# Layer 1 self-attention: the fourth of a head's products with the values issued behind the next head's first scores

## The chip, the cores and the metric

The kernel runs on one core of a Trainium2 chip. The metric is the device time of one execution in microseconds (us). The core has five engines with an instruction queue each: TensorE for matmuls (PE in the profile, its weight loads PEld), VectorE (DVE), ScalarE (ACT), GpSimd (POOL) and SyncE (SP), which issues most of the transfers. The engines run side by side and wait for each other by semaphores.

## The reference, cut to what matters

The program is a two-layer decoder on 4 batches of 512 rows of 512 columns, in float32. Each layer has a self-attention, a cross-attention and a feed-forward part, and each part is added to the rows and followed by a normalisation of the row. The change is in the self-attention of layer 1, which has 16 query heads of 128 columns, four of which share one key and value head, a rotation of queries and keys by position, and a causal mask:

```python
    xqkv = x @ Wqkv
    xq, xk, xv = ...                 # 16 query heads, 4 key and 4 value heads of 128
    xq = apply_rotary_emb(xq)
    xk = apply_rotary_emb(xk)
    scores = jnp.einsum('bqhd,bkhd->bhqk', xq, xk) * scale
    scores = scores + causal_add[None, None]
    probs = jax.nn.softmax(scores, axis=-1)
    attn = jnp.einsum('bhqk,bkhd->bqhd', probs, xv).reshape(B, S, q_size)
    return attn @ Wo
...
    x = _layernorm(x + _L1_attn_ref(x, L1_attn_Wqkv, L1_attn_Wo), axis=-1)
```

## The kernel before, in words

`l1_attn` walks over 64 heads, numbered n = 0 to 63 (batch n // 16, head h = n % 16). Three heads are in work at a time. In the turn of head n the loop writes, for i = 0 to 3: the scores of one block of 128 query rows of head n + 1 (`scores`, L918 to L922: a matmul into `ps_s`, the mask and the row maximum on DVE, the exponential on ACT), one of four products that make the query of head n + 2 (`queries`, L905), the transposes of one block of 128 key columns of head n's probabilities (`turn`, L935, copied out of `ps_t` into `PT` by ACT at L940 for even blocks and by DVE at L938 for odd ones), and the division of head n + 1's finished rows by their sums (`normalise`, L928 and L929). Behind the last query product stands the rotation of that query (`rope`): three DVE instructions, L875 to L877, and one on POOL, L878, which writes `q`.

Then comes `values(n, pts)`: four products of the transposed probabilities with the values, accumulated in one `ps_m` buffer (L950). Causality makes them 512, 384, 256 and 128 columns wide. The fourth, of 128 columns, reads the `PT` block that DVE copies last. ACT copies the sum into the tile `attnT` (L952). When h % 4 is 3, the four heads in `attnT` are multiplied by their part of `Wo` and added to the rows: 16 matmuls of 512 columns, at L160 in the helper `mm`, and four additions at L292. At the start of the turn of head n the loop writes `keys(n + 2)`, which does four matmuls (also at L160) and a rotation if n + 2 is the first of a group of four, and nothing otherwise. So between the turns of head n and n + 1 there stands, besides `values`: nothing more when n % 4 is 0 or 2, the keys of head n + 3 when it is 1, and the projection when it is 3. I call these plain heads, key heads and projection heads. After the last head of a batch come `layernorm(b)` and the values of the next batch (`prep_values`, 16 matmuls at L160, copies at L890).

A float32 matmul of 512 columns shows as two MATMUL records of about 0.43 us each in sequence, and one of 128 columns as two of about 0.11 us.

What sets the order on the engines: from the end of the layer 0 feed-forward until the call of `finish(3)` after head 2, the order on PE, DVE and ACT is the written one (`in_order`, L834). From there to the end of `l1_attn` a planner orders each engine's instructions when the program is built: on each engine it takes, of those that by its own estimate of durations are ready, the one that is written first. The engines then execute that order strictly; the chip does not choose again. The buffers concerned: `ps_m` 3, `ps_s` 3, `ps_t` 2, `PT` 6, `P` 8, `attnT` 1, `tmp` 4.

`at_start` runs `finish(1)` to `finish(3)` after heads 0 to 2 (the ends of the layer 0 feed-forward: scaling on ACT at L841 and on DVE at L842, transposes at L846, a projection, a `layernorm`), and `at_end` runs `begin(0)` to `begin(4)` after heads 59 to 63, which loads and prepares the cross-attention.

Of the kernel before, what the change touches and what calls it, by code (L numbers as in the profile page):

```python
# [17 lines left out]
P = 128  # L18
B, S, F = 4, 512, 512
# [67 lines left out]
def decoder_kernel(ctx: ExitStack, tc: tile.TileContext, a: dict, out: bass.AP):  # L87
# [21 lines left out]
    V, A, G, PE = nc.vector, nc.scalar, nc.gpsimd, nc.tensor  # L109


    def act(tag, free, bufs=1, dtype=F32):
        return ap.tile([P, *free], dtype, tag=tag, name=tag, bufs=bufs)

    def tmp(dtype=F32):
        return tp.tile([P, 512], dtype, tag="tmp", name="tmp")

    def small(n, tag, bufs=2):
        return sp.tile([P, n], F32, tag=tag, name=tag, bufs=bufs)

    def prob(tag, free, bufs, dtype=F32):
        return pools["pp"].tile([P, *free], dtype, tag=tag, name=tag, bufs=bufs)

    def pss():
        return pools["ps_s"].tile([P, 512], F32, tag="s", name="ps_s")
# [6 lines left out]
    def psm(dtype=F32):  # L132
        return pools["ps_m"].tile([P, 512], dtype, tag="m", name="ps_m")
# [7 lines left out]
    def load(src, free):  # L141

        w = weight(free)
        nc.sync.dma_start(w, src)
        return w

    def rows(w):
        return w.rearrange("(k p) n -> p k n", p=P)

    def tk(t):  # L150
        return slice(t * P, (t + 1) * P)
# [4 lines left out]
    def mm(ps, lhs, rhs):  # L156

        n = len(lhs)
        for i, (x, y) in enumerate(zip(lhs, rhs)):
            PE.matmul(ps, lhsT=x, rhs=y, start=(i == 0), stop=(i == n - 1))  # L160
# [54 lines left out]
    def layernorm(b):  # L215
        mv = small(8, "mv")
        for i in range(4):
            st = sp.tile([P, 6], F32, tag="bn", name="bn")
            V.bn_stats(st, X[4 * b + i])  # L219
            V.bn_aggr(mv[:, 2 * i:2 * i + 2], st)  # L220
        rstd = small(4, "rstd")
        A.activation(rstd, mv.rearrange("p (t s) -> p t s", s=2)[:, :, 1], AF.Sqrt, bias=LN_EPS)  # L222
        V.reciprocal(rstd, rstd)
        for i in range(4):
            x = X[4 * b + i]
            V.tensor_scalar(x, x, mv[:, 2 * i:2 * i + 1], rstd[:, i:i + 1], ALU.subtract, ALU.mult)  # L226
# [60 lines left out]
    def add_projection(b, lhs, rhs):  # L287

        for t in range(4):
            ps = psm()  # L290
            mm(ps, [x[:, tk(t)] for x in lhs], rhs)
            V.tensor_tensor(X[4 * b + t], X[4 * b + t], ps, ALU.add)  # L292

    def chunks(w):
        return [w[:, k, :] for k in range(w.shape[1])]
# [565 lines left out]
    def l1_attn(at_start, at_end):  # L861
        cos, sin = prob("cos", [S], 1), prob("sin", [S], 1)
        nc.sync.dma_start(cos, a["k_rope"][0])
        nc.sync.dma_start(sin, a["k_rope"][1])
        wqkv = rows(a["L1_attn_Wqkv"])
        wk = load(wqkv[:, :, 4 * F:5 * F], (4, F))
        wv = load(wqkv[:, :, 5 * F:6 * F], (4, F))
        wq, wo = [None] * 4, [None] * 4
        for of, g in ((wq, 0), (wq, 1), (wo, 0), (wq, 2), (wo, 1), (wq, 3), (wo, 2), (wo, 3)):
            src = wqkv[:, :, g * F:(g + 1) * F] if of is wq else rows(a["L1_attn_Wo"])[:, 4 * g:4 * g + 4, :]  # L870
            of[g] = load(src, (4, F))

        def rope(dst, ps, scale):
            x, y = tmp(), tmp()
            V.scalar_tensor_tensor(x, ps, scale, cos, ALU.mult, ALU.mult)  # L875
            V.scalar_tensor_tensor(y[0:64], ps[64:128], scale, sin[64:128], ALU.mult, ALU.mult)
            V.scalar_tensor_tensor(y[64:128], ps[0:64], scale, sin[0:64], ALU.mult, ALU.mult)  # L877
            G.tensor_tensor(dst, x, y, ALU.add)  # L878

        heads = [(b, h) for b in range(B) for h in range(H1)]
        st, qs, ks, ps_q, ps_sm = {}, {}, {}, {}, {}

        def prep_values(b):
            v = prob("v", [4, F], 1)
            for t in range(4):
                ps = psm()
                mm(ps, [st["xt"][:, k, tk(t)] for k in range(4)], chunks(wv))
                A.copy(v[:, t, :], ps)  # L890
            st["v"] = v

        def keys(n):
            b, h = heads[n]
            if h % 4 == 0:
                ps = psm()
                mm(ps, [wk[:, k, tk(h // 4)] for k in range(4)], chunks(st["xt"]))
                ks[b, h // 4] = prob("k", [S], 3)
                rope(ks[b, h // 4], ps, 1.0)

        def queries(n, i):
            b, h = heads[n]
            if i == 0:
                ps_q[n] = psm()
            PE.matmul(ps_q[n], lhsT=wq[h // 4][:, i, tk(h % 4)], rhs=st["xt"][:, i, :],  # L905
                      start=(i == 0), stop=(i == 3))
            if i == 3:
                qs[n] = prob("q", [S], 3)
                rope(qs[n], ps_q.pop(n), float(D1) ** -0.5)

        def scores(n, qi):
            b, h = heads[n]
            w, q, k = (qi + 1) * P, qs[n], ks[b, h // 4]
            if qi == 3:
                ps_sm[n] = [None] * 4, small(4, "sums", 3), small(4, "nmax", 3)
            probs, sums, nmax = ps_sm[n]
            s = pss()
            PE.matmul(s[:, :w], lhsT=q[:, tk(qi)], rhs=k[:, :w], start=True, stop=True)  # L918
            V.tensor_tensor(s[:, tk(qi)], s[:, tk(qi)], causal_mask, ALU.add)
            V.tensor_reduce(nmax[:, qi:qi + 1], s[:, :w], AX.X, ALU.max, negate=True)  # L920
            p = probs[qi] = prob("P", [S], 8)
            A.activation(p[:, :w], s[:, :w], AF.Exp, bias=nmax[:, qi:qi + 1],  # L922
                         accum_out=sums[:, qi:qi + 1])

        def normalise(n, qi):
            probs, sums, _ = ps_sm[n]
            p, w = probs[qi], (qi + 1) * P
            V.reciprocal(sums[:, qi:qi + 1], sums[:, qi:qi + 1])  # L928
            V.tensor_scalar(p[:, :w], p[:, :w], sums[:, qi:qi + 1], None, ALU.mult)  # L929

        def turn(n, c):
            probs = ps_sm[n][0]
            pt = pst()
            for qi in range(c, 4):
                PE.transpose(pt[:, tk(qi)], probs[qi][:, tk(c)], ident)  # L935
            sb = prob("PT", [S], 6)
            if c % 2:
                V.tensor_copy(sb[:, c * P:], pt[:, c * P:])  # L938
            else:
                A.copy(sb[:, c * P:], pt[:, c * P:])  # L940
            return sb

        def values(n, pts):
            b, h = heads[n]
            g = h // 4
            if h % 4 == 0:
                st["ft"] = act("attnT", [4, S])
            av = psm()
            for c in range(4):
                PE.matmul(av[:, c * P:], lhsT=st["v"][:, c, tk(g)], rhs=pts[c][:, c * P:],  # L950
                          start=(c == 0), stop=(c == 3))
            A.copy(st["ft"][:, h % 4, :], av)  # L952
            if h % 4 == 3:
                add_projection(b, chunks(st["ft"]), chunks(wo[g]))
            del ps_sm[n]

        N = len(heads)
        st["xt"] = transposed(0)
        for n in range(2):
            keys(n)  # L960
            for i in range(4):
                queries(n, i)
        for qi in (3, 2, 1, 0):
            scores(0, qi)
        prep_values(0)
        for qi in (3, 2, 1, 0):
            normalise(0, qi)
        for n, (b, h) in enumerate(heads):
            pts = []
            if n + 2 < N:  # L970
                keys(n + 2)
            for i in range(4):
                qi = 3 - i
                if n + 1 < N:
                    scores(n + 1, qi)
                if n + 2 < N:
                    queries(n + 2, i)
                pts.append(turn(n, i))
                if n + 1 < N and i:
                    normalise(n + 1, qi + 1)  # L980
            values(n, pts)
            if n + 1 < N:
                normalise(n + 1, 0)
            if h == 13 and b + 1 < B:
                st["xt"] = transposed(b + 1)
            if n < 3:
                at_start(n)
            if n >= N - 5:
                at_end(n - N + 5)
            if h == 15:  # L990
                layernorm(b)
                if b + 1 < B:
                    prep_values(b + 1)

# [438 lines left out]
```

## Time and profile before

| what | value |
|---|---|
| median of three runs | 2961.57 us (2957.27 to 2965.47) |
| the profiled execution | 2978.49 us, its span 2976.7 us |
| mean granted TensorE clock | 0.979 |
| PE busy | 2800.3 us, 94% of the span |
| DVE / ACT / POOL busy | 1770.5 / 1059.2 / 337.5 us |
| the stretch of `l1_attn` with the planner's order, 1110 to 1930 us | 820 us, PE busy 803.26, DVE 558.32, ACT 238.75, POOL 88.60 |

The span runs from the first to the last instruction; the profiled execution is 1.8 us longer than its span. Times in a timeline are us from the start of the span. In a row of the timeline there stand the start, the duration, the engine, the line of the code, the operation, what it writes and reads, the count of merged instructions and, in brackets, how long the engine was idle before it and what ended that. PE's matmul durations overlap, so a group's place in time says more than its length.

### The profile page before, as it was taken

Reading aid. Unit: us, or ns where it says so; the run is one execution under the profiler, and the core shown is the slowest. Engines: PE = TensorE matmul, PEld = TensorE weight load, DVE = VectorE, ACT = ScalarE, POOL = GpSimd, SP = SyncE. Lnnn points to the kernel's source line nnn. Section 1 sums busy time; section 2 is a strip of 40 time slices with the busy share of each in tenths; the row PEclk is TensorE's granted clock in tenths of the full one; section 3 lists DMA queues with packets and bytes.
Section 4 is the critical chain, followed back from the end, with each engine's and each line's share of the span. In section 5 each row is a group of like instructions: output and inputs, shape, how many; then the busy total and the mean of one; then the engine's idle time right before and its main releaser. Section 6 shows DMA issues by size and latency. Waiting matters only on the chain. (4 is left out here: it accounts for less than half of the span.)

```text
span 2976.7 us, 30405 instructions
## 1 busy us (share of the span) xinstructions
PE 2800.3 (94%) x11514; PEld 1353.3 (45%) x11514; DVE 1770.5 (59%) x3586; ACT 1059.2 (36%) x1945; POOL 337.5 (11%) x295
## 2 busy tenths in 40 slices
PE   8999999998997989999999999999998999998888
PEld 3444444564563445545555555543333343333443
DVE  4565455543111577766766767656666666564898
ACT  2343342333221222322332322234554544544444
POOL 3000000042004001101111111121211211100000
PEclk9999999999999999999999999999999999999999
DMA  9600000004303020000000000100111010010000
GB/s 383 272 15 0 18 11 14 22 32 143 132 33 114 29 71 1 1 1 1 1 1 0 1 29 22 57 22 29 43 36 43 29 42 23 1 43 1 15 15 29
DMA packets 56453, 131.85 MB, mean 44 GB/s; under 512 B 4809, under 2 KB 24026, under 8 KB 50146
## 3 DMA queue, kind: packets, MB, share of 16 engines
q1 hardware_dynamic: 53218, 121.31, 11.3%
q0 software_dynamic: 3072, 8.39, 0.8%
q8 instruction: 99, 1.62, 0.2%
q14 instruction: 64, 0.52, 0.1%
HBM read 82.76 MB, written 46.92 MB: 44 GB/s over the span
## 5 line engine op out<-in xcount | busy, mean ns | idle before, releaser
L160 PE MATMUL ps_m<-w,attnT 128*128 128x512 f32 (+2 forms) x1216 | 443.2, 515 | 11.8 <-DVE x L292 6.1
L1138 DVE TENSOR_REDUCE maxes<-ps_b 128x2 f32<-128x1024 f32 x256 | 312.0, 1223 | 237.6 <-PE ps_b L1150 212.1
L1154 ACT ACTIVATE PT<-ps_b 128x1024 f32<-128x1024 f32 x256 | 260.7, 1022 | 243.6 <-PE ps_b L1150 241.5
L1150 PE MATMUL ps_b<-q,k 32*128 32x512 f32 x1024 | 293.0, 650 | 16.6 <-DVE maxes L1138 8.5
L1134 PE MATMUL ps_b<-k,q 32*128 32x512 f32 x1024 | 286.4, 644 | 2.3 <-ACT PT L1154 1.8
L160 PEld LDWEIGHTS ps_m<-w,attnT 128*128 128x128 f32 x960 | 182.4, 193 | 189.7 <-issue 171.1
L905 PE MATMUL ps_m<-xT,w 128*128 128x512 f32 x512 | 261.4, 594 | 0.0
L292 DVE TENSOR_TENSOR x<-x,ps_m 128x512 f32<-128x512 f32 x128 | 87.7, 687 | 290.9 <-PE ps_m L160 263.1
L922 ACT ACTIVATE P<-ps_s,nmax 128x512 f32<-128x512 f32 (+3 forms) x256 | 135.2, 528 | 234.4 <-DVE nmax L920 233.4
L918 PE MATMUL ps_s<-k,q 128*128 128x512 f32 (+3 forms) x512 | 184.2, 443 | 18.7 <-POOL q L878 17.1
L878 POOL TENSOR_TENSOR q<-tmp 128x512 f32<-128x512 f32 x64 | 81.2, 1269 | 766.7 <-DVE tmp L877 732.1
L950 PE MATMUL ps_m<-PT,v 128*128 128x512 f32 (+3 forms) x512 | 162.8, 441 | 3.6 <-DVE PT L938 3.6
L349 ACT ACTIVATE P<-ps_s,nmax 128x512 f32<-128x512 f32 x128 | 88.4, 692 | 203.6 <-DVE nmax L347 203.6
L1134 PEld LDWEIGHTS ps_b<-k,q 32*128 32x128 f32 x1024 | 79.0, 185 | 164.4 <-issue 116.5
L929 DVE TENSOR_SCALAR P<-P,sums 128x512 f32<-128x512 f32 (+3 forms) x256 | 150.3, 587 | 5.3
L160 PE MATMUL ps_m<-w,xT 128*128 128x512 f32 (+1 forms) x384 | 143.6, 529 | 3.5 <-DVE v L317 3.5
L1161 PE MATMUL ps_m<-PT,vv 128*32 128x512 f32 x1024 | 139.9, 619 | 4.8 <-ACT PT L1154 4.8
L935 PEld LDWEIGHTS ps_t<-kc,P 128*128 128x128 f32 x640 | 83.9, 141 | 120.7 <-issue 81.7
L950 PEld LDWEIGHTS ps_m<-PT,v 128*128 128x128 f32 x512 | 89.3, 191 | 105.9 <-issue 49.4
L327 PE MATMUL ps_m<-xT,w 128*128 128x512 f32 x256 | 121.3, 600 | 10.9 <-DMA w<-in_L_attn_Wq 10.9
L920 DVE TENSOR_REDUCE nmax<-ps_s 128x1 f32<-128x512 f32 (+3 forms) x256 | 125.5, 490 | 5.6
L160 PE MATMUL ps_m<-xT,w 128*128 128x256 f32 (+1 forms) x384 | 126.6, 469 | 0.8 <-DVE x L292 0.8
(269 smaller groups left out, 4254.7 us busy)
## 6 DMA issues: line engine op xcount, KB each, us to landing
hidden<-w SPq DMA_DIRECT2D x16, 1024.0 KB, 16.9
result<-w SPq DMA_DIRECT2D x16, 1024.0 KB, 16.8
w<-in_L_ffn_gateT SPq DMA_DIRECT2D x8, 1024.0 KB, 4.7
w<-in_L_ffn_upT SPq DMA_DIRECT2D x8, 1024.0 KB, 4.8
w<-in_L_ffn_downT SPq DMA_DIRECT2D x8, 1024.0 KB, 5.0
w<-in_L_attn_Wqkv SPq DMA_DIRECT2D x6, 1024.0 KB, 5.2
w<-in_L_attn_Wo SPq DMA_DIRECT2D x5, 1024.0 KB
result<-P SPq DMA_DIRECT2D x18, 256.0 KB, 2.1
```

The source lines that it names most:

```text
L160: PE.matmul(ps, lhsT=x, rhs=y, start=(i == 0), stop=(i == n - 1))
L905: PE.matmul(ps_q[n], lhsT=wq[h // 4][:, i, tk(h % 4)], rhs=st["xt"][:, i, :], start=(i == 0), stop=(i == 3))
L918: PE.matmul(s[:, :w], lhsT=q[:, tk(qi)], rhs=k[:, :w], start=True, stop=True)
L920: V.tensor_reduce(nmax[:, qi:qi + 1], s[:, :w], AX.X, ALU.max, negate=True)
L922: A.activation(p[:, :w], s[:, :w], AF.Exp, bias=nmax[:, qi:qi + 1], accum_out=sums[:, qi:qi + 1])
L929: V.tensor_scalar(p[:, :w], p[:, :w], sums[:, qi:qi + 1], None, ALU.mult)
L950: PE.matmul(av[:, c * P:], lhsT=st["v"][:, c, tk(g)], rhs=pts[c][:, c * P:], start=(c == 0), stop=(c == 3))
L1134: PE.matmul(s[:, j, :], lhsT=q[strip(i), tk(qi)], rhs=k[strip(i), :], start=True, stop=True)
L1138: V.tensor_reduce(at[:, 2 * half:2 * half + 2, 16 * (1 - g % 2)], s, AX.X, ALU.max, negate=True)
L1150: PE.matmul(s[:, j, :], lhsT=k[strip(i), tk(c)], rhs=q[strip(i), :], start=True, stop=True)
L1154: A.activation(p, s, AF.Exp)
L1161: PE.matmul(avs[g][strip(i), :], lhsT=vv[c][:, 4 * m + i, 16 * par:16 * par + 32], rhs=pts[g, c, i // 2][:, i % 2, :], start=(c == 0), sto ...
```

## The change

`values` becomes a generator. Its first call does the products c = 0, 1 and 2 and stops. The rest (the fourth product, the copy into `attnT`, the projection where h % 4 is 3, and after the last head of a batch the `layernorm` and the values of the next batch) is written in the next head's turn, at i = 0, behind `keys` and the first `scores`, and ahead of the first query product. For head 63 it follows at once. The `attnT` tile is asked for behind the fourth product instead of ahead of the first. No instruction is added or removed.

```diff
         def values(n, pts):
             b, h = heads[n]
             g = h // 4
+            av = psm()
+            for c in range(4):
+                if c == 3:
+                    yield
+                PE.matmul(av[:, c * P:], lhsT=st["v"][:, c, tk(g)], rhs=pts[c][:, c * P:],
+                          start=(c == 0), stop=(c == 3))
             if h % 4 == 0:
                 st["ft"] = act("attnT", [4, S])
-            av = psm()
-            for c in range(4):
-                PE.matmul(av[:, c * P:], lhsT=st["v"][:, c, tk(g)], rhs=pts[c][:, c * P:],
-                          start=(c == 0), stop=(c == 3))
             A.copy(st["ft"][:, h % 4, :], av)
             if h % 4 == 3:
                 add_projection(b, chunks(st["ft"]), chunks(wo[g]))
+            if h == 15:
+                layernorm(b)
+                if b + 1 < B:
+                    prep_values(b + 1)
             del ps_sm[n]
...
+        rest = iter(())
         for n, (b, h) in enumerate(heads):
...
                 if n + 1 < N:
                     scores(n + 1, qi)
+                if i == 0:
+                    next(rest, None)
                 if n + 2 < N:
                     queries(n + 2, i)
...
-            values(n, pts)
+            rest = values(n, pts)
+            next(rest)
             if n + 1 < N:
                 normalise(n + 1, 0)
+            else:
+                next(rest, None)
...
-            if h == 15:
-                layernorm(b)
-                if b + 1 < B:
-                    prep_values(b + 1)
```

## The prediction, made before the change was run

> **What bounds the kernel now.** I read the page first, then the chain of waits of PE, then the timeline of one plain head, one projection head and two single places. From the page:
>
> ```profile
> PE 2800.3 (94%) x11514; PEld 1353.3 (45%) x11514; DVE 1770.5 (59%) x3586; ACT 1059.2 (36%) x1945; POOL 337.5 (11%) x295
> ...
> L918 PE MATMUL ps_s<-k,q 128*128 128x512 f32 (+3 forms) x512 | 184.2, 443 | 18.7 <-POOL q L878 17.1
> ...
> L950 PE MATMUL ps_m<-PT,v 128*128 128x512 f32 (+3 forms) x512 | 162.8, 441 | 3.6 <-DVE PT L938 3.6
> ```
>
> PE is the bound: whatever leaves PE idle or fills its holes moves the end. The wait that the change would cover, that of the fourth product for its `PT` block, is worth 3.6 us of idle PE in all; the scores' wait for the rotated query is worth 17.1. The waits from 990 to 1950 us (engine, line, what it waited for: us, times, longest) say the same in another way:
>
> ```profile
> PEld ps_m L950 <- DVE PT L938: 39.4, 62, 1.8
> ...
> PEld ps_s L918 <- POOL q L878: 23.7, 31, 1.0
> ...
> PE ps_s L918 <- POOL q L878: 17.1, 31, 0.6
> ...
> PE ps_m L950 <- DVE PT L938: 3.6, 6, 1.0
> ```
>
> The weight load waits 62 times for `PT`, but PE itself only 6 times. Why, a plain head (n = 32) shows:
>
> ```profile
> 1532.31 2.10 PE L950 MATMUL ps_m<-PT,v 128*128 128x512 f32 x6
> ...
> 1534.24 1.02 PE L905 MATMUL ps_m<-xT,w 128*128 128x512 f32 x2
> 1534.59 0.29 DVE L938 COPY PT<-ps_t 128x128 f32<-128x128 f32 x1
> 1534.73 1.26 POOL L878 TENSOR_TENSOR q<-tmp 128x512 f32<-128x512 f32 x1 [34.99 <-DVE tmp L877]
> ...
> 1535.10 0.38 PE L950 MATMUL ps_m<-PT,v 128*128 128x128 f32 x2
> ...
> 1536.05 1.12 PE L918 MATMUL ps_s<-k,q 128*128 128x512 f32 x2 [0.56 <-POOL q L878]
> ```
>
> Three products, then the next head's first query product (L905, written later, put ahead by the planner), then the fourth product, then the scores. Counted from the end of the third product (1534.24): `PT` is ready at 0.64, the query product ends at 0.86, so the fourth product starts at once and ends at 1.08. POOL ends at 1.75 and the scores start at 1.81. The hole is 1.81 - 1.08 = 0.73 us, and it belongs to `q`. The projection head n = 39 has no hole, since the projection covers `q` (ready at 1621.36 + 1.27 - 1620.64 = 1.99):
>
> ```profile
> 1620.64 1.02 PE L160 MATMUL ps_m<-w,attnT 128*128 128x512 f32 x2
> ...
> 1621.57 0.49 PE L950 MATMUL ps_m<-PT,v 128*128 128x128 f32 x2
> ...
> 1621.89 13.04 PE L160 MATMUL ps_m<-w,attnT 128*128 128x512 f32 x30
> ...
> 1634.77 1.02 PE L918 MATMUL ps_s<-k,q 128*128 128x512 f32 x2
> ```
>
> **What the Trainium skill says.** "TensorE: Matmul & The Clock Gate", Architectural detail: PE's queue can pull weight loads ahead of running matmuls, while ACT and DVE are strictly first in, first out. The trace agrees: the load of the fourth product waits 0.50 us for `PT` while PE works, and no matmul overtakes another. "GPSIMD Engine Reference", 3.1 Elementwise: a two-input add takes 4497 ns for 2048 elements; a quarter of that is 1.12 us as an estimate, the trace has 1.26 for 512, and that is used. The same page, 1 Specifications: POOL's SBUF interface is shared with VectorE; the division of 256 columns (L929) beside L878 takes 1.34 us against 0.35 elsewhere, yet L878 stays at 1.26, so `q` isn't made later by it.
>
> **The change, part by part.** No instruction is added or taken away, and none of the moved ones issues a DMA; SP's queue waits for nothing here that comes later. The question is only the new order on PE, and whether the planner holds the scores ready earlier than the chip does.
>
> It does. At head 2 DVE has the mask of the next scores ahead of the scaling L842:
>
> ```profile
> 1077.96 1.70 ACT L841 ACTIVATE w<-w,share 128x256 f32<-128x256 f32 x4
> ...
> 1079.23 0.30 DVE L919 TENSOR_TENSOR ps_s<-ps_s,kc 128x128 f32<-128x128 f32 x1 [0.67 <-PE ps_s L918]
> ...
> 1079.43 1.66 DVE L842 SCALAR_TENSOR_TENSOR w<-w,share 128x256 f32<-128x256 f32 x4
> ```
>
> L842 is written earlier, and on the chip its first input was ready at 1077.96 + 0.43 = 1078.39, 0.84 us before the mask could start. The planner put it second, so in its plan `q` comes at least some 0.8 us earlier against the chain `PT`, fourth product, L952, L841 than on the chip (1.11 after `PT`), so within some 0.3 to 0.4 of `PT`. That supposes that the scaled rows' gather is not late in the plan. And when is `PT` ready in the plan? At head 61 five transposes of 0.11 us, which are written later, stand ahead of the fourth product, so at about 0.44 to 0.55 behind the third (0.90 on the chip; key and projection heads run 0.23 later than plain ones). So planned `q` is at about 0.5 to 0.7 in a plain head and 0.6 to 0.95 in a projection head, as estimates. Behind the third product neither the scores nor the fourth product is planned ready, so the filler stays: the query product or the first projection matmul, to 0.86. Then the planner chooses, and now the scores are written first.
>
> - Plain heads from n = 4 to 60, 29 of them: query product, scores, fourth product. The scores can't start before 1.81 whatever stands ahead. The fourth product leaves the hole, where it cost nothing, and its 0.22 us goes behind the scores, ahead of the work that leads to the next query. 29 x 0.22 = +6.4 us.
> - Projection heads, n = 3 to 59, 15 of them: the scores move from behind the projection into it. From the end of the third product to that of the scores and all 16 projection matmuls PE has 16 x 0.86 + 0.22 + 0.86 = 14.84 us of work, and took 1634.77 + 0.86 - 1620.64 = 14.99. With the scores at 0.86 PE waits until 1.99 + 0.05 = 2.04, 1.18 us instead of 0.15: +1.03. With the fourth product first (it ends at 1.14) it waits 0.90 + 0.06: +0.81. I take 0.9: 15 x 0.9 = +13.5 us.
> - Key heads, n = 5 to 61, 15 of them: the four key matmuls (3.44 us) cover both `PT` and `q`. Before, the scores started 3.82 behind the third product, with 3.66 of work: 0.16 idle. That goes: -2.4 us.
> - Heads 0 and 1, in the written order: the fourth product waited while PE would be idle for L842 anyway (1.69 and 1.74 us), so leaving costs and gains nothing there. But the copy into `attnT` is now queued on ACT between the exponential of the first scores and the `PT` copy that PE awaits (1044.26 and 1071.71, PE idle 3.32 and 1.89 us): 0.48 us each, +1.0 us. Head 2's fourth product is free of the written order; nothing.
> - `layernorm` and `prep_values` inside the generator, three times: the same instructions behind one score block. The square root's table load and the one back (1.28 us each) are one pair as before and lie beside 13.8 us of PE work; without that cover 3 x 1.28.
> - Buffers: the sum in `ps_m` is held up to 2 us longer. The other two are the next query's sum and one that the rotation has left by then (L877 ends at 0.5 to 0.75), so nothing waits; if PE did wait for a slot it would be for the rest of L877, under 0.1 us a head, either way inside the range. `attnT` asked for later: nothing, since its readers ended a head earlier.
>
> Sum: 6.4 + 13.5 - 2.4 + 1.0 = +18.5 us. Against the profiled execution: 2978.49 + 18.5 = 2997.0. That execution stands 0.57% above the median of the runs; the addition is the same there, so I forecast 2961.57 + 18.5 = 2980 us.
>
> **The rivals.**
>
> 1. The planner's `q` is later than I infer, over 0.86 in plain and over 1.14 in projection heads. Then plain heads stay as they are, and in projection heads another projection matmul fills to 2.0, when `q` is there. Left: -2.4 + 1.0, that is 2960 us. For it: only the bound of 1.08 for plain heads is firm, since nothing was put between the fourth product and the scores. Against it: head 2. Here the change doesn't do what it says.
> 2. In between: `q` planned at 0.86 to 1.08, plain heads stay, projection heads put the scores behind the fourth product: 15 x 0.81 - 2.4 + 1.0 = +10.8, 2972 us.
> 3. Faster: with neither the scores nor the fourth product planned ready at 0.86, a second query product (0.86 us) goes into the plain heads' hole, which then is 1.81 - 0.86 = 0.95 wide. It would save 0.73 us in 29 heads, 21 us, 2940 us; it decides from 13 heads on (8.9 / 0.73). For it: the hole is there, and the product needs nothing but `xT` and weights. Against: before, the fourth product was always chosen at 0.86, so it was planned ready.
> 4. Slower still: DVE's load shifts and the planner puts the 256-column division ahead of the rotation in plain heads too, as it does in the others (0.23 us later): 29 x 0.23 = +6.7 on top, 2987 us.
>
> **How the numbers follow.** A measurement can tell about 0.3%, 8.9 us, from no change: 2952.7 to 2970.5. Forecast with either order in projection heads (2976 to 2983): 0.52. Rival 1: 0.21. Rival 2: 0.11, of which a fifth may fall within 0.3%. Rival 3: 0.11. Rival 4: 0.05. So slower 0.66, same 0.23, faster 0.11. The range takes the forecast and rivals 1, 2 and most of 4, with the run to run spread of 4 us: 2956 to 2988; the slower cases alone span 2968 to 2988.
>
> **What the profile after would show.** In plain heads L918 ahead of the 128-column L950, with an idle time of about 0.95 us before it, and that head longer by 0.22. In projection heads L918 behind one L160 matmul, idle for 0.9 to 1.2 us, and the sum of the waits of L918 for `q` up from 17 us to some 30 (its own part of the hole, without the weight load's). Key heads: L160 times 8 without the L950 between. The idle before L950 for `PT` at almost nothing. The prediction is wrong if in the projection heads L918 still comes late enough for `q`, or if a longer filler than one matmul stands ahead of it.

## The result and the profile after

The changed kernel is slower: 2989.0 us median against 2961.48 (a fourth run of the kernel before has joined the three of the table), a ratio of 1.0087 with a 95% interval of 1.0074 to 1.0100, so about 26 us, and 27.5 by the medians.

The two profiled executions differ by only 12.4 us (spans 2976.7 and 2989.1). The one of before took 21 us longer up to the first product of head 0 (1019.54 against 998.11 us), in work that the change doesn't touch; in the runs below this part takes 994 to 1019 us. From there to the first product of head 63 (1960.87 and 1966.86) the stretch went from 941.33 to 968.75 us: +27.4, which is what the medians show. What follows took 6.4 us longer after the change (1022.2 against 1015.8); it takes 1015 to 1026 us in the runs below, so that isn't told from noise. All comparisons of traces below are made inside this stretch.

Inside the stretch PE was busy 911.3 us before and 911.8 after, at a mean granted clock of 0.99 both times, so the loss is idle time of PE, and its waiting for `q` grew. The rows of the page after that answer to the three shown of before:

```profile
PE 2801.1 (94%) x11492; PEld 1356.9 (45%) x11514; DVE 1777.7 (59%) x3586; ACT 1054.6 (35%) x1945; POOL 338.4 (11%) x295
...
L918 PE MATMUL ps_s<-k,q 128*128 128x512 f32 (+3 forms) x512 | 185.4, 445 | 45.2 <-POOL q L878 43.6
...
L950 PE MATMUL ps_m<-PT,v 128*128 128x512 f32 (+3 forms) x512 | 159.8, 436 | 0.0
```

The fourth product's wait for `PT` went from 3.6 us to nothing; the scores' wait for `q` went from 17.1 to 43.6. The waits from 990 to 1985 us (engine, line, what it waited for: us, times, longest):

```profile
PEld ps_s L918 <- POOL q L878: 81.0, 49, 2.1
...
PE ps_s L918 <- POOL q L878: 43.4, 49, 1.3
```

They were 31 waits before (one of them ahead of head 0) and are 49 now: the 15 projection heads have joined, and with them the key heads n = 13, 29 and 45 and head 61. The plain head n = 32 and the projection head n = 39 in the timeline:

```profile
1525.66 2.10 PE L950 MATMUL ps_m<-PT,v 128*128 128x512 f32 x6
...
1527.59 1.02 PE L905 MATMUL ps_m<-xT,w 128*128 128x512 f32 x2
1527.94 0.29 DVE L938 COPY PT<-ps_t 128x128 f32<-128x128 f32 x1
1528.08 1.26 POOL L878 TENSOR_TENSOR q<-tmp 128x512 f32<-128x512 f32 x1 [36.11 <-DVE tmp L877]
...
1529.40 1.13 PE L918 MATMUL ps_s<-k,q 128*128 128x512 f32 x2 [0.78 <-POOL q L878]
...
1530.36 0.39 PE L950 MATMUL ps_m<-PT,v 128*128 128x128 f32 x2
```

```profile
1616.09 1.02 PE L160 MATMUL ps_m<-w,attnT 128*128 128x512 f32 x2
1616.67 0.29 DVE L938 COPY PT<-ps_t 128x128 f32<-128x128 f32 x1
1616.81 1.26 POOL L878 TENSOR_TENSOR q<-tmp 128x512 f32<-128x512 f32 x1 [8.87 <-DVE tmp L877]
...
1618.12 1.13 PE L918 MATMUL ps_s<-k,q 128*128 128x512 f32 x2 [1.01 <-POOL q L878]
1619.09 0.38 PE L950 MATMUL ps_m<-PT,v 128*128 128x128 f32 x2
```

In the plain head `PT` is ready 0.63 us behind the third product (1527.60) and PE is free at 0.86, but the scores are next in its queue, and it waits for `q` until 1.80 with the fourth product, which could run, standing behind them. In the projection head the same wait lasts from 1616.95 to 1618.12. The fourth product could have run in it (`PT` is there at 1616.96), and so could the next two projection matmuls of 0.86 us, which read earlier heads in `attnT`. Of all 16 only the four that multiply head 39 itself need the fourth product first.

Measured from the first product of one head to that of the next, the heads fall into a few groups, and within a group they agree to 0.02 us, head 42 aside (0.48):

| heads | scores start behind the third product, before and after | change per head | sum |
|---|---|---|---|
| plain, all others (18) | 1.80, 1.80 | +0.22 | +3.9 |
| plain, behind one of the 11 key heads below (11) | 1.80, 2.03 | +0.45 | +5.0 |
| projection, n = 7 to 59 (14), and n = 3 | 14.13 (27.86 at a batch's end), 2.03; at n = 3 15.27, 2.30 | +1.11, +0.32 | +15.8 |
| key (11) | 3.82, 3.43 | -0.17 | -1.9 |
| key at n = 13, 29, 45 (3) | 5.99, 2.04 | +0.68 | +2.0 |
| n = 61, and n = 0 to 2 | 4.62, 2.07 at n = 61 | | +0.6, +2.0 |

The sums make the 27.4 us. In the three key heads of the fifth row the scores now stand among transposes of the next batch's rows (L233), and wait; in head 13:

```profile
1225.53 1.13 PE L918 MATMUL ps_s<-k,q 128*128 128x512 f32 x2 [0.45 <-POOL q L878]
```

### The profile page after: what moved, and what is told of

It reads as the page before. It is cut to its first block, busy times and chain, and to the rows that moved or that the text cites. A ratio compares the mean times of both kernels' runs of the same rounds, so it can differ in the third digit from the quotient of the medians.

```text
span 2989.1 us, 30383 instructions
## 1 busy us (share of the span) xinstructions
PE 2801.1 (94%) x11492; PEld 1356.9 (45%) x11514; DVE 1777.7 (59%) x3586; ACT 1054.6 (35%) x1945; POOL 338.4 (11%) x295
## 5 line engine op out<-in xcount | busy, mean ns | idle before, releaser
L918 PE MATMUL ps_s<-k,q 128*128 128x512 f32 (+3 forms) x512 | 185.4, 445 | 45.2 <-POOL q L878 43.6
L919 DVE TENSOR_TENSOR ps_s<-ps_s,kc 128x128 f32<-128x128 f32 x256 | 75.3, 295 | 127.1 <-PE ps_s L918 127.1
L954 ACT COPY attnT<-ps_m 128x512 f32<-128x512 f32 x64 | 37.4, 585 | 296.3 <-PE ps_m L950 296.3
L940 ACT COPY PT<-ps_t 128x512 f32<-128x512 f32 (+1 forms) x128 | 61.2, 478 | 218.7 <-PE ps_t L935 218.7
```

## The experiments

Two theories. The order theory: only the place on PE matters; the scores, which stand in PE's order earlier than the chip has `q`, are now ahead of work that could fill the wait. The holding theory: the sum in `ps_m` is held longer and the copy into `attnT` and all behind it come later, and each postponed head pays for that alike, 27.5 / 63 = 0.44 us. The sizes that the expectations give the order theory are those of the table above; what these runs test is whether they stay with their kind of head. Ratios are to the kernel before, run beside each kernel on the same chip; the chips differ, so medians of different groups (2977 us, 2978 us and 2961 us for the kernel before) are not compared.

**Postponing one kind of head at a time.** The changed kernel, with the rest of the other kinds done at once. Projection heads at once:

```diff
             rest = values(n, pts)
             next(rest)
+            if h % 4 == 3:
+                next(rest, None)
```

> Projection heads (n % 4 = 3) do their rest at once, all other heads as in the change. Order theory (the loss is the place of the scores on PE ahead of the rest): plain heads keep +0.22 us each (29 heads, 6.4), the plain heads behind a key head +0.23 more (11 heads, 2.5), key heads -0.17 (11) and +0.68 (3), heads 0 to 2 +2: about +11 us, 2972 us, ratio 1.004. Holding theory (every postponed head costs the same because the sum's buffer and the copy into attnT come later, 27.5 / 63 = 0.44 us a head): 48 heads, +21 us, 2982 us.

Ratio 1.0033 (1.0021 to 1.0045), some 10 us. Then only the projection heads postponed (`if h % 4 != 3:` in the same place):

> Only projection heads postpone their rest. Order theory: 14 heads at +1.11 us and head 3 at +0.3: about +16 us, 2977 us, ratio 1.005; the scores wait some 1.2 us for q behind one projection matmul, and heads 15, 31 and 47, which carry the normalisation and the next values, cost no more than the others. Holding theory: 15 heads at 0.44, +6.6 us, 2968 us.

Ratio 1.0052 (1.0039 to 1.0065), 15.5 us. Only the plain heads (`if h % 4 in (1, 3):`):

> Only plain heads (n % 4 = 0 or 2) postpone their rest. Order theory: +0.22 us in 29 heads and a little in heads 0 and 2, about +7 us, 2968 us; the scores still start 1.80 us behind the third product, and no plain head has the extra 0.23, since the 256-column division goes ahead of the rotation only behind key heads that are postponed. Holding theory: 32 heads at 0.44, +14 us, 2975 us.

Ratio 1.0024 (1.0015 to 1.0033), 7 us. Only the key heads (`if h % 4 != 1:`):

> Only key heads (n % 4 = 1) postpone their rest. Order theory: -0.17 us in 11 of them, +0.23 in the 11 plain heads behind them, +0.68 in heads 13, 29 and 45, +0.5 in head 1: about +3 us, 2964 us, not to be told from no change. Holding theory: 16 heads at 0.44, +7 us, 2968 us. A forecast of this study's prediction, the 0.16 us saved in each key head alone, would give -2.4 us, 2959 us.

Ratio 1.0007 (0.9999 to 1.0016), 2 us, not told from no change. The four follow the order theory, and a price that is the same for every head is out: at 0.44 us each the 15 projection heads would cost 6.6 us and the 48 others 21, and they cost 15.5 and 10. In the traces the effect stays in its heads. With only projection heads postponed each of n = 7 to 59 takes +1.11 us, heads 15, 31 and 47 too, so the moved normalisation and next values cost nothing, and all other heads from n = 4 on are unchanged to 0.01 (heads 0 to 2 moved by +0.8 together). PE's waits from 1110 to 1930 us, with the projection heads postponed alone, and then with the projection heads at once:

```profile
PE ps_s L918 <- POOL q L878: 30.1, 42, 1.1
PE ps_m L950 <- DVE PT L938: 1.0, 3, 0.3
```

```profile
PE ps_s L918 <- POOL q L878: 25.9, 31, 1.0
```

14 waits more than the 28 of the plain heads in the one, and 3 more in the other (heads 13, 29 and 45).

The key heads alone settle the 0.23 us that appears in plain heads behind them. DVE in such a head, n = 10, before, and then with only key heads postponed:

```profile
1195.19 0.15 DVE L928 RECIPROCAL sums<-sums 128x1 f32<-128x1 f32 x1
1195.31 0.69 DVE L875 SCALAR_TENSOR_TENSOR tmp<-ps_m,cos 128x512 f32<-128x512 f32 x1
```

```profile
1192.22 0.16 DVE L928 RECIPROCAL sums<-sums 128x1 f32<-128x1 f32 x1
1192.42 0.35 DVE L929 TENSOR_SCALAR P<-P,sums 128x256 f32<-128x256 f32 x1
1192.69 0.68 DVE L875 SCALAR_TENSOR_TENSOR tmp<-ps_m,cos 128x512 f32<-128x512 f32 x1
```

The planner put the 256-column division ahead of the rotation, and `q` and the scores follow 0.23 us later. Why it does so isn't shown. With only plain heads postponed it isn't there: all 29 plain heads take +0.22.

**The rest ahead of the scores.** All of the change, but two statements exchanged:

```diff
-                if n + 1 < N:
-                    scores(n + 1, qi)
                 if i == 0:
                     next(rest, None)
+                if n + 1 < N:
+                    scores(n + 1, qi)
```

> Everything of the change (the split, the held sum, the late attnT tile, projection, normalisation and next values in the next head's turn, behind the keys), but the rest written ahead of the first scores instead of behind them. Order theory: plain and projection heads as in the kernel before, key heads -0.17 us, plain heads behind them +0.23 by the division ahead of the rotation: within 3 us of the kernel before, 2962 us. Holding theory: most of the 27 us stays, over 2980 us.

Ratio 0.9994 (0.9983 to 1.0004): the loss is gone with the sum still held over the keys and all that was moved still in the next turn. In the trace plain and projection heads from n = 4 on are as before, key heads -0.17 and plain heads behind them +0.24. The projection head n = 55, with the scores again at 14.13 behind the third product:

```profile
1852.68 1.02 PE L160 MATMUL ps_m<-w,attnT 128*128 128x512 f32 x2
1853.61 0.49 PE L950 MATMUL ps_m<-PT,v 128*128 128x128 f32 x2
...
1866.81 1.02 PE L918 MATMUL ps_s<-k,q 128*128 128x512 f32 x2
```

So it is the place behind the scores that costs. In plain and projection heads, though, the rest runs here where it ran before, so for them this exchange doesn't show that holding the sum is free. The next two runs bear on that.

**The wait itself.** POOL's addition in two parts, first the 128 columns that the first scores read, put into the changed kernel and into the kernel before:

```diff
-        def rope(dst, ps, scale):
+        def rope(dst, ps, scale, parts=(slice(0, S),)):
...
-            G.tensor_tensor(dst, x, y, ALU.add)
+            for c in parts:
+                G.tensor_tensor(dst[:, c], x[:, c], y[:, c], ALU.add)
...
-                rope(qs[n], ps_q.pop(n), float(D1) ** -0.5)
+                rope(qs[n], ps_q.pop(n), float(D1) ** -0.5, (tk(3), slice(0, 3 * P)))
```

> The changed kernel with POOL's addition of the rotated query in two parts, the 128 columns that the first scores read ahead of the other 384. If the wait for q is what the changed order pays for: q's first part is there 0.8 us earlier (estimate: a quarter of 1.26 us and the issue), so plain heads lose 0.8 us of idle PE (29 heads, -24) and projection heads too (15, -12): about -37 us against the changed kernel, 2951 us, below the kernel before. If the loss comes from holding the sum and the late copy, the same two-part addition brings about -21 us, as in the kernel before, and the distance of 27 us between the two stays: 2967 us.

> The kernel before with POOL's addition in the same two parts, nothing postponed. The hole of 0.73 us in 29 plain heads closes (the scores start at the end of the fourth product, 1.08 us behind the third): -21 us, 2940 us, ratio 0.993. If something else stands behind q in the plain heads' hole, less than half of it.

The changed kernel with it: ratio 0.9960 (0.9945 to 0.9974), some 38 us less than without it by the two ratios, where 37 were expected. The kernel before with it: 0.9940 (0.9920 to 0.9961), 2959.29 against 2978.17 us, faster than both kernels. The plain head n = 32 of the latter (the lines are numbered one higher in these two kernels):

```profile
1518.09 2.10 PE L951 MATMUL ps_m<-PT,v 128*128 128x512 f32 x6
...
1520.03 1.02 PE L906 MATMUL ps_m<-xT,w 128*128 128x512 f32 x2
1520.38 0.29 DVE L939 COPY PT<-ps_t 128x128 f32<-128x128 f32 x1
1520.52 1.46 POOL L879 TENSOR_TENSOR q<-tmp 128x128 f32<-128x128 f32 x2 [34.85 <-DVE tmp L877]
...
1520.88 0.38 PE L951 MATMUL ps_m<-PT,v 128*128 128x128 f32 x2
...
1521.10 1.04 PE L919 MATMUL ps_s<-k,q 128*128 128x512 f32 x2
```

The scores follow the fourth product at once, at 1.07 instead of 1.80. The same head of the changed kernel with two parts:

```profile
1525.99 1.02 PE L906 MATMUL ps_m<-xT,w 128*128 128x512 f32 x2
...
1526.99 1.12 PE L919 MATMUL ps_s<-k,q 128*128 128x512 f32 x2
1527.95 0.39 PE L951 MATMUL ps_m<-PT,v 128*128 128x128 f32 x2
```

Here the scores start at 1.00 in 18 plain heads, and at 1.23 in the 11 behind a key head and in the projection heads, which then cost +0.30 instead of +1.11. The distance between the orders, heads 3 to 61, falls from 25.5 us to 7.5 (-11.4 and -18.9 against before): most of the loss was the wait for `q`. What stays is 0.21 us in 25 plain heads (5.4; n = 4, 16, 32 and 48 take the same in both), where the fourth product no longer runs while PE waits, and 0.30 in 14 projection heads (4.2), less 2.1 that the key heads and n = 61 save. The gain of the better version is 18 us and not 21: 14 plain heads save 0.81, but 15 only 0.56 (the 11 behind a key head and n = 4, 16, 32 and 48), and n = 13, 29 and 45 take 0.30 longer. In heads 10 and 32 the next transposes start 0.22 us behind the end of the scores, after a division beside POOL (0.83 us for 128 columns) is done. That reading is from the trace alone.

**Without the planner.** PE, DVE and ACT in the written order to the end of the stage, for both kernels (the lines are numbered two lower in them):

```diff
-            if b == B - 1:
-                in_order.close()
...
     l1_attn(lambda n: finish(n + 1), begin)
+    in_order.close()
     run()
```

> The kernel before with PE, DVE and ACT in the written order through all of the stage, no planner. Then the fourth product waits for PT with nothing in between: plain heads idle 0.69 for PT and 0.89 for q, 1.58 instead of 0.73; key and projection heads idle 0.92 instead of 0.1: 30 x 0.85 + 31 x 0.8 = about +50 us, 3011 us. If the planner's filler is worth nothing: no change.

> The changed kernel in the written order. Here the change does what its words say: no wait for PT at all. But the scores stand straight behind the third product and wait for q: plain heads 1.80 us (+0.22 against the kernel before in written order), key heads nothing (-0.9), projection heads 2.03 instead of 0.92 (+1.1): 30 x 0.22 - 15 x 0.9 + 15 x 1.1 = about +10 us against the kernel before in written order. If the planner's wrong idea of q is the only reason for the loss, the change gains here, by up to 61 x 0.7 = 43 us.

Ratios 1.0217 (1.0189 to 1.0245) and 1.0248 (1.0221 to 1.0274), medians 3026.06 and 3034.96 us. The planner's order is worth some 64 us to the kernel before, where 50 were expected; in heads 3 to 61 the trace has 51, and most of the rest is in heads 0 to 2. The intervals of the two overlap; inside the stretch from head 0 to 63 the change costs 12.8 us in the traces, and 8.9 by the medians. PE's waits from 1080 to 2000 us, the kernel before in written order, then the changed one:

```profile
PE ps_m L948 <- DVE PT L936: 37.5, 58, 0.7
PE ps_s L916 <- POOL q L876: 18.0, 29, 0.6
```

```profile
PE ps_s L916 <- POOL q L876: 77.0, 44, 1.8
```

Here is the wait that the change aims at, 58 times 0.65 us, and the change removes it. It doesn't pay even so: 15 projection heads wait for `q` for the first time. Against before in written order plain heads take +0.22, projection heads +1.11 and key heads -0.91 us (n = 13, 29 and 45 +0.22). So the loss doesn't need a planner with a wrong idea of `q`: scores that are written first stand in the way just the same.

## Why the prediction was right, and where its sizes were off

Direction and mechanism were right, the size was too small: +18.5 forecast, +27.5 by the medians, which is one microsecond above the top of the range (2988); by the ratio it is 26. Of the 9 us that were missing in the stretch, 3.1 belong to the key heads, 2.5 to the division, 2.4 to the projection heads and 1.0 to heads 0 to 2.

- Plain heads, +0.22 in 29: measured 0.22, with the scores at 1.80 as said. Shown by postponing them alone.
- Projection heads, taken at 0.9: measured 1.11 in 14 heads, 15.8 instead of 13.5 us in all. The term mis-sized is the choice between the two orders, where I took the middle: the planner put the scores first in every one. The sum for that order, +1.03, left out that the first scores take 0.97 us instead of 0.86 when PE has waited for them (1618.12 to 1619.09 in head 39): their weight load starts with them then, at 1618.12, and ran 0.43 us ahead of them in the kernel before. The 0.15 us lost before was read about right: 0.07 ahead of the fourth product and 0.10 in it. So 1.17 + 0.11 - 0.17 = 1.11.
- Key heads, -0.16 in 15: -0.17 in 11 of them. In heads 13, 29 and 45 it failed, +0.68 each. There the keys wait for the transposes of the next batch's rows, and the scores got between these and waited for `q`. The step counted these three with the others, and also head 61, behind which no keys stand, since there is no head 64: +0.56.
- The division ahead of the rotation was rival 4, at 0.05 and with 29 heads. It came in 11 heads, those behind a key head that is postponed, as shown above: +2.5 us.
- Heads 0 to 2, +1.0: measured +2.0 in one trace. Head 0 took 0.52 longer, where 0.48 was forecast, but it took 0.51 less in the kernel that leaves these heads unchanged, and the three together 0.8 more there. So the forecast is neither shown nor refuted.
- The inference on the planner, that it holds `q` ready by the end of one filler, fits the orders that it chose: in every plain head from 4 to 60 the scores stand behind one query product and ahead of the fourth product. The planner's own times stand in no run, so its reason stays inferred. Rivals 1 to 3 didn't occur.
- The sum of the scores' waits for `q`, forecast at some 30 us: 43.4. The forecast has only the projection heads in it. In plain heads the part that is listed at the scores rose too, from 0.56 to 0.78 us and to 1.01 behind a key head, since the fourth product no longer runs ahead of them.
- `layernorm` and `prep_values` at nothing: held, by heads 15, 31 and 47. Buffers at nothing: no wait of its own shows; the exchange of the two statements has the sum held over the keys at no loss, and with `q` in two parts what stays of the distance is accounted for by the order on PE.

## What to carry to other kernels

A wait in the list of the weight loads is not yet idle time of PE: the same wait was 39.4 us there and 3.6 us on the matmuls, because a filler stood in it. Before work is moved behind something, ask what that something itself waits for; here the scores' query came 1.1 us later than the block they were to cover. Where an engine's order is fixed ahead, an instruction that stands in it before its input is there blocks everything behind it, whoever put it there, so look for such a case in the trace (an instruction idle at the head of its queue with ready work behind) before giving it a better place; making the awaited piece smaller gained 0.6% where moving the work lost 0.9%.

## What the runs showed that I had not expected

POOL's addition in two parts, 128 and 384 columns, took 1.46 us together against 1.26 in one. And a change on PE and ACT alone reordered DVE a head later: with the key heads' fourth product and its copy moved, a 0.35 us division went ahead of the rotation in the next plain head, 0.23 us in each of 11, though no DVE instruction was written in another place.
